# A perceiver layer on one core: the beginning of the score phase by a written plan, projections in pairs, and context parts made a step further ahead

## The chip, the core and the metric

The kernel runs on one core of a Trainium2 chip. TensorE (PE) multiplies, VectorE (DVE) does elementwise arithmetic and reductions, ScalarE (ACT) copies, casts and exponentials, GpSimd (POOL) a few reductions over partitions, SyncE (SP) issues nearly all transfers, which 16 DMA engines carry out. Each engine takes its instructions in the order in which the program gives them to it, and waits on semaphores of the others. The metric is the device time of the whole program in microseconds (us), lower is better: the median of several runs.

## The reference: what is computed

One layer of a perceiver. `x` is 128 rows of 512 numbers, the context is 12544 rows of 512. There are three residual parts:

```python
x = x + cross_attention(layernorm(x), context)      # 16 heads of 128, softmax over 12544 rows
x = x + linear_attention(layernorm(x))              # 16 heads of 32, gated
x = x + ffn(layernorm(x))                           # 512 -> 2048 -> 512, weights and inputs quantized
```

Only the first is touched by the change. Its scores are `(x Wq) (context Wk)^T / sqrt(128)`, for all heads, and its output is `softmax(scores) (context Wv) Wo`.

The kernel never projects the context. It takes Wk to the query side, so that each head's query becomes a vector of 512 numbers, and weighs the raw context with the exponentials before Wv is applied. All large products are done in a fast float32 form with operands split into a high and a low part: `a b` becomes `lo hi + hi lo + hi hi`, three matmuls.

## The kernel before

**Prologue** (lines 171 to 276). The query rows are normalised (`layernorm`, L105), transposed (L198, L199) and projected. Heads are taken in eight pairs, `h2` from 0 to 7. For each pair, `load_w` (L173) loads 512 KB of query weights `wq` and 512 KB of key weights `wk`; `project_q` (L201) makes `pq` in PSUM, and ACT scales it into `qT` (L213); `project_k` (L216) multiplies `qT` with the key weights into `pk`, and ACT copies `pk` out in two halves (L230) into the buffers `b`. There are two buffers for `pq` and two for `pk`. On PE the order is q0, q1, k0, q2, k1, and so on.

The first four head pairs are called f = 0, the other four f = 1. From the `b` of each, seven operands are made for a Strassen-Winograd product: B11, T2, T3, T1, T4, B21, B22 (`operands`, L236). `put` (L232) casts one to its high part on ACT and subtracts it on DVE for the low part. They stay in SBUF, in rooms named `kq0_n` and `kq1_n` for the two f. The other side, the context transposed, comes in pieces of two row blocks: `load_ct` (L147) loads 512 KB, `sum_ct` (L155) makes four sums of it on DVE, `split_ct` (L162) the high parts on ACT and the low parts on DVE.

**Score units** (`scores`, L293). A unit is one context piece i of 49 with one f. It makes seven products of six 128x512 matmuls each (L300), p1, p6, p7, p5, p4, and then p2 added onto p1 and p3 added onto p5 in their PSUM banks. DVE combines them: u2 (L319), u3 (L322), c22 (L325), c21 (L328), c12 (L338); ACT copies p1 out twice (L316, L334). p3 can't begin before DVE has read p5 for c22. The unit's scores, 1 MB, go to DRAM (L339), and DVE keeps a running maximum (L332, L343). During the first units, `more` puts what is left of the f = 1 operands between DVE's steps (L283 to L287, L318 and on). There are 98 units.

**Context steps** (L566 to L606). 196 steps, two to a unit, f = 0 first. Step k takes 24 matmuls (`weigh`, L355, records at L362) with the exponentials of half a unit's scores as one operand (`ph` and `pl`, high and low) and half a context piece as the other (`ch` and `cl`). A step takes PE 24 times 226.7 ns, 5.44 us. Around it, in the order of L586 to L595, stand: `high_part` of step k+2, `cut_hi` (makes `ch`), `low_part` of step k+1 (makes `pl`), `soften` of k+3 (DVE subtracts the maximum, ACT takes the exponential, in place in `si`), `cut_lo` of k+1 (makes `cl`), `total` of k+1 (DVE adds up the denominator `lsum`), the load of the scores of k+5 and that of the context of k+3. `ch`, `cl` and the two loads happen in every other step. `pl` has two buffers. Beside them, jobs are hung on certain steps (`at`, L538), among them a reduction over partitions on POOL (`all_over`, L551) of the f = 0 denominators at step 104.

**Change of phase** (L435 to L469). Before the last unit, `soften`, `cut_hi` and `high_part` of step 0 are given out, and the rest of step 0 and parts of step 1 during it, through `more`. The scores and context of the second pair of steps are loaded after it.

**What sets the order.** Instructions are recorded in the order of the program text, and a scheduler then may move them within each engine; those in `seq(...)` (`keep_in_program_order`, L74) stay in the order in which they are given among themselves. In the prologue and in the units most are free before the change.

**The tail** (L610 and on) does the rest of the layer. The change doesn't touch its text.

Of the kernel before, what the change touches and what calls it, by code (L numbers as in the profile page):

```python
# [8 lines left out]
F32 = mybir.dt.float32  # L9
# [7 lines left out]
P = 128  # L17
# [16 lines left out]
def tile_perceiver_layer(  # L34
# [111 lines left out]

    def load_ct(i):  # L147
        if i == 1:
            raw = kq1p.tile([P, 8, 2, P], F32, name=f"kq1_{B22}")
        else:  # L150
            raw = ctp.tile([P, 8, 2, P], F32, tag="raw", name="ctr", bufs=1)
        nc.sync.dma_start(out=raw[:, A11:, :, :], in_=cT[i])
        return raw

    def sum_ct(raw):  # L155
        r = lambda s: raw[:, s, :, :]
        nc.vector.tensor_tensor(r(S1), r(A21), r(A22), ALU.add)
        nc.vector.tensor_tensor(r(S3), r(A11), r(A21), ALU.subtract)
        nc.vector.tensor_tensor(r(S2), r(S1), r(A11), ALU.subtract)
        seq(nc.vector.tensor_tensor(r(S4), r(A12), r(S2), ALU.subtract))  # L160

    def split_ct(raw, lo=None):  # L162
        hi = ctp.tile([P, 7, 2, P], F32R, tag="hi", name="cth")
        if lo is None:
            lo = ctp.tile([P, 7, 2, P], F32R, tag="lo", name="ctl")
        nc.scalar.copy(hi, raw[:, :7, :, :])
        nc.vector.tensor_tensor(lo, raw[:, :7, :, :], hi, ALU.subtract)
        return hi, lo


    with tc.tile_pool(name="ps_pro", bufs=2, space=PSUM) as ps_pro:

        def load_w(h2):  # L173

            hs = slice(h2 * 256, (h2 + 1) * 256)
            if h2 in (2, 3):
                both = kq1p.tile([P, 2, 1024], F32, name=f"kq1_{h2 + 2}")
                wq = both[:, 0, :].rearrange("p (c e) -> p c e", c=NC)
                wk = both[:, 1, :].rearrange("p (h d) -> p h d", h=2)
            else:  # L180
                wq = ctp.tile([P, NC, 256], F32, tag="hi", name="wq")
                wk = ctp.tile([P, 2, D], F32, tag="lo", name="wk")
            nc.sync.dma_start(out=wq, in_=x_wq[:, hs].rearrange("(c p) e -> p c e", p=P))
            nc.sync.dma_start(out=wk, in_=x_wkT[hs, :].rearrange("(h p) d -> p h d", p=P))
            return wq, wk

        keep_warm(ps_pro, 9)
        ws = [load_w(h2) for h2 in range(4)]
        raw = load_ct(0)
        xn = mxp.tile([P, D], F32, tag="mx1", name="xn")  # L190
        layernorm(xn, x0, D)

        warm = const.tile([P, 1], F32, name="warm")
        seq(nc.scalar.activation(warm, x0[:, 0:1], AF.Exp))
        xnT = tmp.tile([P, NC, P], F32, tag="u3", name="xnT")
        pt = ps_pro.tile([P, NC, P], F32, tag="q", name="pt")
        for i in range(NC):
            nc.tensor.transpose(pt[:, i, :], xn[:, i * P : (i + 1) * P], ident)  # L198
        nc.vector.tensor_copy(xnT, pt)  # L199

        def project_q(h2):  # L201
            pq = ps_pro.tile([P, 2, P], F32, tag="q", name="pq")
            for j in range(2):
                for cc in range(NC):
                    nc.tensor.matmul(  # L205
                        pq[:, j, :],
                        lhsT=ws[h2][0][:, cc, j * HD : (j + 1) * HD],
                        rhs=xnT[:, cc, :],
                        start=(cc == 0),
                        stop=(cc == NC - 1),  # L210
                    )
            qT = tmp.tile([P, 2, P], F32, tag=("p1", "u2")[h2 % 2], name="qT")
            nc.scalar.mul(qT, pq, HD**-0.5)  # L213
            return qT

        def project_k(h2, qT, b):  # L216

            pk = ps_pro.tile([P, 2, 2, 256], F32, tag="k", name="pk")
            for cc in range(NC):
                for j in range(2):  # L220
                    nc.tensor.matmul(  # L221
                        pk[:, cc // 2, cc % 2, j * P : (j + 1) * P],
                        lhsT=ws[h2][1][:, j, cc * P : (cc + 1) * P],
                        rhs=qT[:, j, :],
                        start=True,
                        stop=True,
                    )
            o = h2 % 2 * 256
            for a in range(2):
                nc.scalar.copy(b[h2 // 2 % 2][:, a, :, o : o + 256], pk[:, a, :, :])  # L230

        def put(f, s, v):  # L232
            nc.scalar.copy(right(f, s, 0), v)
            nc.vector.tensor_tensor(right(f, s, 1), v, right(f, s, 0), ALU.subtract)  # L234

        def operands(f, b):  # L236

            (b11, b21), (b12, b22) = ((t[:, 0, :, :], t[:, 1, :, :]) for t in b)
            t2 = mxp.tile([P, 2, 512], F32, tag=f"mx{f}", name="t2")
            sub = lambda out, x, y: nc.vector.tensor_tensor(out, x, y, ALU.subtract)  # L240
            return [
                lambda: sub(b11, b12, b11),
                lambda: sub(t2, b22, b11),
                lambda: put(f, T2, t2),
                lambda: sub(b12, b22, b12),
                lambda: put(f, T3, b12),
                lambda: put(f, T1, b11),
                lambda: sub(b21, b21, t2),
                lambda: put(f, T4, b21),
                lambda: put(f, B22, b22),  # L250
            ]

        qT = project_q(0)
        for h2 in range(8):
            if h2 + 4 < 8:
                ws.append(load_w(h2 + 4))
            if h2 == 1:
                raw1 = load_ct(1)
            nxt = project_q(h2 + 1) if h2 + 1 < 8 else None
            if h2 % 4 == 0:  # L260
                b = [iop.tile([P, 2, 2, 512], F32, tag="io", name="b") for _ in range(2)]
            project_k(h2, qT, b)
            qT = nxt
            if h2 == 1:
                put(0, B11, b[0][:, 0, :, :])
                put(0, B21, b[0][:, 1, :, :])
            if h2 == 2:
                sum_ct(raw)
            if h2 == 3:
                rest = operands(0, b)  # L270
                for do in rest[:6]:
                    do()
            if h2 == 5:
                cts = {0: split_ct(raw, mbp.tile([P, 7, 2, P], F32R, name="mb"))}
                for do in rest[6:]:
                    do()
# [3 lines left out]
    mx = [mxp.tile([P, 1024], F32, name=f"mx{f}") for f in range(2)]  # L280
    psx = ExitStack()
    ps_s = psx.enter_context(tc.tile_pool(name="ps_s", bufs=8, space=PSUM, reuse_waits="tile"))
    beside = operands(1, b)  # L283
    beside[6:6] = [lambda: put(1, B21, b[0][:, 1, :, :])]
    beside[:0] = [
        lambda: (sum_ct(raw1), cts.update({1: split_ct(raw1)})), lambda: put(1, B11, b[0][:, 0, :, :]),
    ]  # L287

    def more():
        if beside:  # L290
            beside.pop(0)()

    def scores(i, f, hi, lo):  # L293


        def product(ps, a, b, first):
            n = 0
            for cc in range(2):
                for lt, part in ((lo, 0), (hi, 1), (hi, 0)):
                    nc.tensor.matmul(  # L300
                        ps, lhsT=lt[:, a, cc, :], rhs=right(f, b, part)[:, cc, :], start=(first and n == 0), stop=(n == 5),
                        skip_group_check=True,
                    )
                    n += 1
            return ps

        def bank():
            return ps_s.tile([P, 512], F32, tag="s", name="ps")

        so = iop.tile([P, 2, 1024], F32, tag="io", name="so")  # L310
        c11, c12, c21, c22 = (so[:, j, b * 512 : (b + 1) * 512] for j in range(2) for b in range(2))
        p1s = tmp.tile([P, 512], F32, tag="p1", name="p1s")
        u2 = tmp.tile([P, 512], F32, tag="u2", name="u2")
        u3 = tmp.tile([P, 512], F32, tag="u3", name="u3")
        p1 = product(bank(), A11, B11, True)
        nc.scalar.copy(p1s, p1)  # L316
        p6 = product(bank(), S2, T2, True)
        more()  # L318
        nc.vector.tensor_tensor(u2, p6, p1s, ALU.add)  # L319
        more()  # L320
        p7 = product(bank(), S3, T3, True)
        nc.vector.tensor_tensor(u3, p7, u2, ALU.add)  # L322
        more()
# [7 lines left out]
        if i > 0 and not late:  # L331
            nc.vector.tensor_tensor(mx[f], mx[f], so[:, 1, :], ALU.max)  # L332
# [675 lines left out]
```

## Time and profile before

| what | value |
|---|---|
| median of 3 runs | 2135.51 us (2135.2 to 2136.2) |
| profiled execution | 2136.68 us |
| its span | 2135.0 us |
| PE busy | 2121.8 us |
| DVE busy | 1658.6 us |
| ACT busy | 762.9 us |
| matmuls L300 on the chain, 4080 | 925.12 us |
| first matmul of the context steps | at 972.74 us |
| first matmul of the tail | at 2040.94 us |
| HBM read and written | 245.77 MB and 103.02 MB |

The profile is that of one execution. Its span is the time from its first to its last instruction, 1.7 us less than the device time of the same execution. Times of single instructions are counted from the span's start. A projection matmul appears as two records on PE, a score or context matmul as one; a record's duration is longer than the distance to the next, because matmuls are pipelined. Idle time of an engine other than PE costs nothing unless PE waits for that engine.

### The profile page before, as it was taken

Reading aid. Unit: us, or ns where it says so; the run is one execution under the profiler, and the core shown is the slowest. Engines: PE = TensorE matmul, PEld = TensorE weight load, DVE = VectorE, ACT = ScalarE, POOL = GpSimd, SP = SyncE. Lnnn points to the kernel's source line nnn. Section 1 sums busy time; section 2 is a strip of 40 time slices with the busy share of each in tenths; the row PEclk is TensorE's granted clock in tenths of the full one; section 3 lists DMA queues with packets and bytes.
Section 4 is the critical chain, followed back from the end, with each engine's and each line's share of the span. In section 5 each row is a group of like instructions: output and inputs, shape, how many; then the busy total and the mean of one; then the engine's idle time right before and its main releaser. Section 6 shows DMA issues by size and latency. Waiting matters only on the chain.

```text
span 2135.0 us, 24185 instructions
## 1 busy us (share of the span) xinstructions
PE 2121.8 (99%) x9627; PEld 1748.9 (82%) x9627; DVE 1658.6 (78%) x1824; ACT 762.9 (36%) x843; POOL 23.5 (1%) x16
## 2 busy tenths in 40 slices
PE   8999999999999999999999999999999999999999
PEld 7888888888888888888888888888888888888885
DVE  6877777777777777778997888877787777777735
ACT  5222122221222212215444444444544444444423
POOL 0000000000000000000000000000000000000010
PEclk9999999999999999999999999999999999999999
DMA  6444443444444444446664555554434444444460
GB/s 221 150 170 160 173 178 154 166 160 170 178 152 171 159 168 178 158 158 227 211 230 152 176 178 180 194 182 144 148 138 140 146 148 148 148 142 145 147 191 25
DMA packets 77393, 350.36 MB, mean 164 GB/s; under 512 B 8000, under 2 KB 12352, under 8 KB 51808
## 3 DMA queue, kind: packets, MB, share of 16 engines
q1 hardware_dynamic: 77136, 348.69, 45.5%
q8 instruction: 75, 1.23, 0.2%
q14 instruction: 38, 0.31, 0.0%
q10 hardware_dynamic: 144, 0.13, 0.0%
HBM read 245.77 MB, written 103.02 MB: 163 GB/s over the span
## 4 chain that ended last, share of the span: by engine, by line
PE 97%; DVE 2%; DMA 1%; issue 1%; ACT 0%; DVEq 0%; SPq 0%
PE pu L362 49%; PE ps L300 43%; PE pw L92 1%; PE pc L631 1%; PE po L652 0%; DMA kq<-in_cT_dram 0%; PE pp L742 0%; DVE kq L234 0%; DMA kq<-in_a_wq_dram 0%; PE pq L205 0%; DVE b L240 0%; PE po L795 0%; PE py L939 0%; PE pk L221 0%; PE pv L766 0%
## 5 line engine op out<-in xcount | busy, mean ns | idle before, releaser
L300 PE MATMUL ps<-kq,cth 128*128 128x512 f32 x2744 | 844.9, 389 | 0.0
L362 PE MATMUL pu<-ph,cl 128*128 128x512 f32 x1568 | 610.2, 389 | 1.4 <-DVE cl L404 1.2
L362 PE MATMUL pu<-ph,ch 128*128 128x512 f32 x1568 | 610.0, 389 | 0.0
L362 PE MATMUL pu<-pl,ch 128*128 128x512 f32 x1568 | 610.0, 389 | 0.0
L300 PEld LDWEIGHTS ps<-kq,cth 128*128 128x128 f32 x2744 | 515.2, 188 | 106.7
L300 PE MATMUL ps<-kq,ctl 128*128 128x512 f32 x1344 | 522.8, 389 | 0.0
L421 DVE TENSOR_TENSOR pl<-si,ph 128x1024 fp32r<-128x1024 f32 x194 | 241.3, 1244 | 203.3 <-PE pu L362 201.6
L362 PEld LDWEIGHTS pu<-ph,cl 128*128 128x128 f32 x1568 | 294.3, 188 | 63.2 <-DVE cl L404 2.2
L362 PEld LDWEIGHTS pu<-pl,ch 128*128 128x128 f32 x1568 | 294.3, 188 | 61.2
L362 PEld LDWEIGHTS pu<-ph,ch 128*128 128x128 f32 x1568 | 294.3, 188 | 61.0
L416 ACT CAST ph<-si 128x1024 fp32r<-128x1024 f32 x194 | 204.0, 1051 | 389.6 <-PE pu L362 389.5
L300 PEld LDWEIGHTS ps<-kq,ctl 128*128 128x128 f32 x1344 | 252.3, 188 | 52.4
L334 ACT COPY so<-ps 128x512 f32<-128x512 f32 x98 | 57.8, 589 | 577.0 <-PE ps L300 577.0
L411 ACT ACTIVATE si<-si 128x1024 f32<-128x1024 f32 x194 | 205.3, 1058 | 116.7 <-DVE si L410 116.7
L410 DVE TENSOR_TENSOR si<-si,mb 128x1024 f32<-128x1024 f32 x194 | 236.6, 1220 | 0.0
L429 DVE TENSOR_TENSOR lsum<-lsum,si 128x1024 f32<-128x1024 f32 x192 | 234.1, 1219 | 0.0
L338 DVE TENSOR_TENSOR so<-ps,u 128x512 f32<-128x512 f32 x98 | 67.8, 691 | 72.3 <-PE ps L300 72.3
L343 DVE TENSOR_TENSOR mx<-mx,so 128x1024 f32<-128x1024 f32 x95 | 116.4, 1225 | 9.6
L404 DVE TENSOR_TENSOR cl<-cr,ch 128x1024 fp32r<-128x1024 f32 x98 | 119.6, 1220 | 0.5 <-ACT ch L398 0.5
L332 DVE TENSOR_TENSOR mx<-mx,so 128x1024 f32<-128x1024 f32 x95 | 116.5, 1227 | 3.2
L398 ACT CAST ch<-cr 128x1024 fp32r<-128x1024 f32 x98 | 103.3, 1054 | 40.8 <-DMA cr<-in_c_dram 40.8
L328 DVE TENSOR_TENSOR so<-ps,u 128x512 f32<-128x512 f32 x98 | 67.7, 691 | 61.2 <-PE ps L300 61.2
(203 smaller groups left out, 1012.4 us busy)
## 6 DMA issues: line engine op xcount, KB each, us to landing
sc<-so SPq DMA_DIRECT2D x98, 1024.0 KB, 3.8
si<-sc SPq DMA_DIRECT2D x97, 1024.0 KB, 4.8
cr<-in_c_dram SPq DMA_DIRECT2D x98, 512.0 KB, 3.5
ctr<-in_cT_dram SPq DMA_DIRECT2D x94, 512.0 KB, 3.5
kq<-in_w1T_dram SPq DMA_DIRECT2D x16, 512.0 KB, 4.8
kq<-in_w2T_dram SPq DMA_DIRECT2D x16, 512.0 KB, 4.9
wq<-in_x_wq_dram SPq DMA_DIRECT2D x6, 512.0 KB, 5.4
wk<-in_x_wkT_dram SPq DMA_DIRECT2D x6, 512.0 KB, 6.2
```

What stands on the lines that cost most here:

```text
L300: nc.tensor.matmul(ps, lhsT=lt[:, a, cc, :], rhs=right(f, b, part)[:, cc, :], start=(first and n == 0), stop=(n == 5), skip_group_check=True,)
L332: nc.vector.tensor_tensor(mx[f], mx[f], so[:, 1, :], ALU.max)
L338: nc.vector.tensor_tensor(c12, p5, u2, ALU.add)
L343: nc.vector.tensor_tensor(mx[f], so[:, 1, :] if i == 0 else mx[f], so[:, 0, :], ALU.max)
L362: nc.tensor.matmul(pu[b][cc], lhsT=lt[:, j, cs], rhs=rt[:, bs], start=(first and n == 0), stop=(last and n == 2))
L398: seq(nc.scalar.copy(ctx_hi[f, i], ctx_raw[f, i]))
L404: seq(nc.vector.tensor_tensor(ctx_lo[f, i], ctx_raw[f, i], ctx_hi[f, i], ALU.subtract))
L410: seq(nc.vector.tensor_tensor(exps[k], exps[k], mb[f], ALU.subtract))
L411: seq(nc.scalar.activation(exps[k], exps[k], AF.Exp))
L416: seq(nc.scalar.copy(high[k], exps[k]))
L421: seq(nc.vector.tensor_tensor(low[k], exps[k], high[k], ALU.subtract))
L429: seq(nc.vector.tensor_tensor(lsum[f], lsum[f], exps[k], ALU.add))
```

## The change

The prologue and the first four units, (0,0), (1,0), (0,1), (1,1) as (i, f), are no longer placed by the scheduler: a text names every step, each step is a small function, and all are kept in the order of the text. Six things differ:

1. The normalisation is written out: two halves of 256 columns, transposed into two PSUM buffers, the first copied out by ACT, the second by DVE.
2. Projections come in pairs on PE: q0 q1 k0 k1 q2 q3 k2 k3 and so on. The copies out of `pk`, called c0a, c0b to c7a, c7b, are placed one by one, some of them much later.
3. The loads are issued in another order: wq0, wq1, wk0, wk1, then wq2, wk2, the first context piece, wq3, wk3, then wq4, wk4, the second context piece, and the rest. The weights of pairs 2, 3, 5 and 6 go to rooms that f = 1 operands will take later, wq7 to that of a maximum; the last block of f = 1 is kept in the room of T4. 
4. The units' body becomes a table of named steps (`unit`); the later units run through it in the order as before.
5. At the change of phase, `soften` and `high_part` of step 1 come before the last unit, `cut_lo` of step 0, `low_part` of steps 0 and 1 within it, and the loads of the second pair of steps before and within it.
6. In the context steps `low_part` and `cut_lo` work for step k+2 instead of k+1, `pl` has three buffers, and the context is loaded for k+4 instead of k+3.

The context piece of a unit is now kept in `raws`, so that it is loaded once for both f; before, from i = 2 on, it was loaded again for f = 1 (L450).

The plan, and the steps that it names (cut to the core; `put` and `operands` of before became the steps h.., l.. and T..):

```diff
+    plan = """
+        q0 q1 qT0 k0 qT1 k1 c0a c0b q2 c1b hB210 lB210 q3 qT2 c1a hB110 S01 S00 k2 S02 qT3 lB110 S03 k3 c2b c2a hi0
+        S11 q4 S10 S12 S13 c3b lo0 ct2 c3a q5 qT4 hB220 T10 k4 qT5 hi1 T30 k5 T20 hT10 lo1 hT30 q6 c4b c5a T40 q7 qT6
+        hT20 lB220 c5b k6 lT20 qT7 hT40 lT30 k7 c6a lT40 c6b c4a lT10 u00p1 c7a hB111 u00p6 c7b lB111 hB221 u00p7 T11
+        u00p1s u00U2 hT11 u00p5 u00U3 hB211 u00p4 u00c22 T21 u00p2 u00c21 hT21 T31 u00p3 u00c11 lT21 hT31 u10p1 u00c12
+        lT31 u10p6 u10p1s lB221 u10p7 u10U2 u10p5 u10U3 S20 u10p4 u10c22 lB211 u10p2 T41 u10p3 u10c21 hT41 lT11 u10c11
+        u01p1 lT41 u01p6 u01p1s u10c12 u00m2 u01p7 u01U2 u01p5 u01U3 S22 u01p4 u01c22 S21 S23 u01p2 u01c21 u10m1 u01p3
+        u01c11 u10m2 u11p1 hi2 u01c12 u01m2 u11p6 u11p1s lo2 u11p7 u11U2 u11p5 u11U3 u11p4 u11c22 u11p2 u11c21 u11m1
+        u11p3 u11c11 u11c12 u11m2
+    """
...
+        room = {2: B11, 3: B21, 5: T3, 6: T1}
+        if h2 in room:
+            both = spare(room[h2], [P, 2, 1024])
...
+            if h2 == 7:
+                wq = mxp.tile([P, NC, 256], F32, tag="mx1", name="wq")
...
+    ws = [load_w(h2) for h2 in range(4)]
+    begin(ws[0][2][0], ws[1][2][0], ws[0][2][1], ws[1][2][1], *ws[2][2])
+    raws[0] = load_ct(0)
+    begin(*ws[3][2])
...
+    for half in range(2):
+        hs = slice(half * 256, (half + 1) * 256)
+        seq(nc.vector.tensor_scalar(xn[:, hs], x0[:, hs], mv[:, 0:1], r, ALU.subtract, ALU.mult))
+    for half in range(2):
+        pt = ps_pro.tile([P, 2, P], F32, tag="q", name="pt")
+        for n in range(2):
+            c0 = (2 * half + n) * P
+            seq(nc.tensor.transpose(pt[:, n, :], xn[:, c0 : c0 + P], ident))
+        to = xnT[:, 2 * half : 2 * half + 2, :]
+        seq(nc.vector.tensor_copy(to, pt) if half else nc.scalar.copy(to, pt))
...
+    for h2 in range(4, 8):
+        ws.append(load_w(h2))
+        begin(*ws[h2][2])
+        if h2 == 4:
+            raws[1] = load_ct(1)
...
+    def leave(h2, a):
+        o = h2 % 2 * 256
+        seq(nc.scalar.copy(block(h2 // 2, a)[:, :, o : o + 256], pks[h2][:, a, :, :]))
...
+    for name in plan.split():
+        if name == "u00p1":
+            pro.close()
+            ps_s = psx.enter_context(tc.tile_pool(name="ps_s", bufs=8, space=PSUM, reuse_waits="tile"))
+        steps_.pop(name)()
```

The change of phase and the context steps:

```diff
     def low_part(k):
         if k < len(steps):
-            low[k] = weigh_operand("pl", 2)
+            low[k] = weigh_operand("pl", 3)
...
+            load_scores(2)
             soften(0)
             cut_hi(0)
             high_part(0)
-            beside = [
-                lambda: None, lambda: None, lambda: cut_lo(0), lambda: None,
-                lambda: low_part(0), lambda: (soften(1), high_part(1)),
-            ]
-        if i + 1 not in cts and i + 1 < NP and i > 0:
-            raw = load_ct(i + 1)
...
+            soften(1)
+            high_part(1)
+            beside = {
+                "U2": [lambda: cut_lo(0), lambda: load_ctx(2)],
+                "c22": [lambda: low_part(0)],
+                "c21": [lambda: low_part(1)],
+            }
+        if i + 1 not in cts and i + 1 < NP and i + 1 not in raws:
+            raws[i + 1] = load_ct(i + 1)
...
-    load_scores(2)
-    load_ctx(2)
...
+        soften(2)
         total(0)
-        soften(2)
         load_scores(4)
...
             high_part(k + 2)
             cut_hi(k + 2)
-            low_part(k + 1)
             soften(k + 3)
-            cut_lo(k + 1)
+            cut_lo(k + 2)
+            low_part(k + 2)
             total(k + 1)
...
             load_scores(k + 5)
-            load_ctx(k + 3)
+            load_ctx(k + 4)
```

## The prediction

> **What bounds the kernel now.** I read the page first: span, then busy shares.
>
> ```profile
> span 2135.0 us, 24185 instructions
> PE 2121.8 (99%) x9627; PEld 1748.9 (82%) x9627; DVE 1658.6 (78%) x1824; ACT 762.9 (36%) x843; POOL 23.5 (1%) x16
> ```
>
> TensorE (PE) is busy for all but 13.2 us. Its matmul count is the same after the change (no matmul is added or removed), and in the steady stretches 128x512 matmuls follow each other every 226.7 ns whatever the other engines do (chain: 4080 of L300 in 925.12 us). So the change can only move PE's idle time. The waits of PE, longest first, say whom it waited for, in us:
>
> ```profile
> PE pk L221 <- ACT qT L213: 1.4, 1, 1.4
> ...
> PE pu L362 <- DVE cl L404: 1.2, 1, 1.2
> PE ps L300 <- ACT b L230: 1.0, 1, 1.0
> PE pq L205 <- DVE xnT L199: 0.8, 1, 0.8
> ...
> PE ps L300 <- DVE so L325: 0.7, 1, 0.7
> ```
>
> Each happens once. The timeline of PE (start, duration, in brackets the idle time before) places them:
>
> ```profile
> 7.10 3.84 PE L205 MATMUL pq<-xnT,wq 128*128 128x128 f32 x32 [0.78 <-DVE xnT L199]
> ...
> 35.56 2.05 PE L221 MATMUL pk<-qT,wk 128*128 128x128 f32 x16 [1.39 <-ACT qT L213]
> ...
> 40.03 0.50 PE L300 MATMUL ps<-kq,mb 128*128 128x512 f32 x1 [1.02 <-ACT b L230]
> ...
> 47.79 0.50 PE L300 MATMUL ps<-kq,mb 128*128 128x512 f32 x1 [0.66 <-DVE so L325]
> ```
>
> Measured from start to start (idle time counts from modelled ends, and the first matmul after a wait takes 0.11 longer), they cost: before the last key projection 35.56-34.01 = 1.55; before the second product 1.42-0.23+0.11 = 1.30; before the seventh product 1.05-0.23+0.11 = 0.93. Later two more: at 983.41 to 983.94, 0.53-0.23+0.11 = 0.41, and at 1549.60 to 1551.20, 1.60-0.23+0.11 = 1.48. The last one's reason is in the timelines of POOL and DVE:
>
> ```profile
> 1543.26 6.12 POOL L554 PARTITION_ALL_REDUCE mb<-lsum  x1 [94.77 <-DVE lsum L553]
> ```
>
> ```profile
> 1544.43 4.45 DVE L421 TENSOR_TENSOR pl<-si,ph 128x1024 fp32r<-128x1024 f32 x1 [1.34 <-PE pu L362]
> 1548.80 1.21 DVE L410 TENSOR_TENSOR si<-si,mb 128x1024 f32<-128x1024 f32 x1
> 1549.94 1.21 DVE L404 TENSOR_TENSOR cl<-cr,ch 128x1024 fp32r<-128x1024 f32 x1
> ```
>
> The same subtraction usually takes 1.22; beside the reduction it took 4.45, and `cl`, third in the queue, came too late. All these waits together with a later start are 0.75+1.55+1.30+0.93+0.41+1.48 = 6.4 us (the 0.75 is worked out below): the ceiling, 0.30%. Last, the transfers of the first 70 us (40 slices of 1.75 us, busy tenths and rate):
>
> ```profile
> DMA  0899999999999918827207271000095000292000
> GB/s 0 262 358 314 354 384 381 367 396 365 372 372 372 298 65 270 240 98 219 81 0 211 89 229 70 0 0 0 0 374 225 9 5 0 112 407 84 0 0 0
> ```
>
> They are saturated up to 24.5. Issue plus time to landing gives, in order of issue: 3.5 (x), 5.0, 7.1, 8.8, 10.1, 11.6, 13.0, 14.5, 15.8, 17.1, 18.6, 20.6, 22.1, 23.4, 24.7. A load of 512 KB lands every 1.5 us on average, in order of issue, whether it is a query weight, a key weight or context.
>
> **What the Trainium skill says.** "TensorE: Matmul & The Clock Gate", section "Architectural detail: the array is 16× 32×32, not 1× 128×128", calls ScalarE and VectorE strict FIFO; the trace agrees: `qT` of the last pair ran at 35.10, behind a 1.70 us cast and three more, though its input had been ready since 32.3. "SBUF — State Buffer", section "Who interferes with whom", says that a `tensor_tensor` with both inputs in SBUF contends with GpSimd's reads and that the one to issue second blocks; 4.45 for 1.22 agrees. "DMA: Bandwidth & Descriptors", section "Queues, rings and completion order", says that descriptors of a ring are consumed in order; the landings agree.
>
> **The change, part by part.** A projection is 16 records, 1.785 us (start to start, 8.90 to 10.69 and on). I follow PE.
>
> Start. The normalisation goes in halves, and so do transpose and copy. The kernel's own later layer does this already (L731, L717): from the first half's start (2070.94) transposes start after 0.47, ScalarE's copy after 0.94 and ends after 1.31. From 5.00 this gives 6.31, first projection at 6.35 instead of 7.10: 0.75 earlier. The other half's copy, on DVE, ends after 1.69, at 6.69; PE needs it after four more matmuls, at 7.24.
>
> Projections. New order q0 q1 k0 k1 q2 q3 k2 k3 and on; loads in the order wq0 wq1 wk0 wk1 wq2 wk2 ct0 wq3 wk3 wq4 wk4 ct1 wq5 wk5 wq6 wk6 wq7 wk7. Five projections end at 6.35+8.93 = 15.28, each load there in time. q3 needs the ninth load, 15.81: it starts at 15.85, 0.57 of waiting. q3 k2 k3 q4 end at 22.99; q5 needs the fourteenth load, 23.40: 0.46 more. q5 k4 k5 q6 q7 end at 23.45+8.93 = 32.38. So the transfers eat 1.03, more than the earlier start gave. On SP's queue the moved loads wait for: wq4 q0 (8.1; it was issued at 9.18 before), wk4 k0 (11.7; 12.76 before). Five loads are then still outstanding, and the others take rooms of the second pair's operands, which wait for no matmul. So the queue stays full, and I keep the landings by position.
>
> Last projections, from ScalarE's new queue. k6 takes the PSUM room of k5, and c5b, which empties it, stands behind qT6 and hT20. q6 ends at 30.59; qT6 starts at 30.79 (copies start 0.31 after the last record's start), holds the queue for 0.28, hT20 for 0.95, c5b takes 0.59: 32.61, k6 at 32.65. k7 takes the room of k6 in turn: k6 ends at 34.43, c6a starts at 34.63, c6b at 35.11 and ends at 35.70: k7 at 35.74, a wait of 1.31 that was not there, in place of the 1.55 for `qT`. Then k7 to 37.62, first product to 38.98. The second product needs the bank that c7b empties, behind c7a (0.48) and hB111 (0.95): 37.82+1.43+0.59 = 39.84, so it starts at 39.9. Before it started at 40.03. From there on: the seventh product waits for c22 on DVE. DVE now has only u2, u3 and c22 (0.69 each) between the fifth product's end, about 44.3, and its need at 46.8, so the 0.93 go. The second pair's operands are due from 57.6 on; DVE's nine remaining passes of 1.14 fit between 45 and 60, the last due at 63. Prologue: 0.13+0.93 = 1.06 gained.
>
> Change of phase (983). `si`, `ch`, `ph`, `pl` of steps 0 and 1 move into the last score unit, and two loads ahead of it. `cl` of step 2 then stands fourth in DVE's row after the last unit instead of ninth (the row from 973.54) and ends near 979; PE needs it at 971.7+10.9 = 982.6. The work moved fills DVE's idle time in that unit (0.74 at 972.9, 0.45 at 968.6, 0.32 at 967.5); the subtractions of steps 0 and 1 now stand ahead of u2, and with the same durations c22 of that unit still ends 0.7 before its need. Gain 0.41.
>
> Context steps. `cl` and `pl` are made two steps ahead instead of one, with a third `pl` buffer. In an ordinary step `cl` ended 3.5 us into a step of 5.44 (1524.95+1.22 against PE's release at 1522.67), 1.9 to spare; the reduction costs DVE 3.23, hence the wait. With another step of 5.44 to spare it is covered: gain 1.48. DVE's work per step is unchanged (3 or 4 passes of 1.14). The context load now follows its reader in the same step and has 10 us; it had about 5.
>
> Context for the scores is loaded once per pair instead of twice (46 loads of 512 KB fewer). Hidden before and after: no wait on it is listed on PE. Worth 0.
>
> Sum: 1.06+0.41+1.48 = 2.95. The profiled execution took 2136.68 (span 2135.0 and 1.7 around it); 2133.7 after. The median of the runs is 2135.51; after it 2132.6, a gain of 0.14%.
>
> **Rivals.** *Loads no limit.* If the ninth and fourteenth load land 1 us earlier than by position, the 1.03 goes, less what ScalarE's order gives back: 3.9 us, 2131.6; with one of the two PSUM waits (1.31, 0.9) halved as well it passes 4.3, 2130.8. For it: the first loads ramp up slowly. Against: 370 GB/s throughout.
>
> *Loads later.* From q3 on PE has no slack against them, so each microsecond costs one. Landings 2.95 later than by position make the kernel slower than before; 7.2 later by over 0.2%, some 2140. Speaks for it: SP is one queue, and wk4, which waits for k0, stands ahead of ten loads; the twelfth load took 2.0. Against: 7 us of transfers are queued when it is issued.
>
> *The lead is not real.* `cl` also waits for the room of the pair before, free only when PE enters the step. If DVE gets no further ahead, 1.48 stays: 2134.0. Against: the room is free a full two steps before the need.
>
> *The prologue gives nothing* and only the 1.9 of the later phases remain: 2133.6.
>
> **How the numbers follow.** Likeliest (0.62): 1.5 to 4.2 us gained. Faster rival 0.17; lead or prologue void 0.15; slower 0.06. 0.2% is 4.3 us, about what a measurement of this kernel can tell from no change: so faster 0.17, within 0.77, slower 0.06. Range: down to 2130.4, which leaves 0.10 of the faster case out, and up to 2135.3, which leaves the slower case and little else. The tail's half-clock stretch (granted clock 0.50 from 2090.08 to 2096.9) can fall otherwise; the three runs span 1.0, inside the range.
>
> **What would show it.** Right: PE's waits of `qT`, `so` and `cl` gone from the list; in their place a wait on a query load near 15, one near 23, one on the copy out of `pk` near 35 (1.3) and one near 39 (0.8); second product at 39.9; first `pu` at 971.7 instead of 972.74; none at 980 or 1550. Wrong: PE reaching the second product before 38.5 (loads no limit) or after 42 (loads late), or a new wait inside the units.

## The result, and the profile after

| what | before | after |
|---|---|---|
| median | 2135.73 us (22 runs, 2133.36 to 2137.95) | 2131.53 us (22 runs, 2129.99 to 2134.30) |
| ratio after to before | | 0.9984, 95% interval 0.9978 to 0.9990 |
| profiled execution, its span | 2136.68, 2135.0 | 2134.19, 2132.5 |
| first matmul of the context steps | 972.74 | 974.19 |
| from there to the first matmul of the tail | 1068.20 | 1066.24 |
| tail (from there to the end) | 94.0 (6.83 us of it at half clock) | 92.0 (3.41 us of it at half clock) |
| HBM read | 245.77 MB | 221.65 MB |

The change takes 0.16% off: 3.4 us by the ratio, 4.2 by the medians, where 2.95 were forecast. That is more than forecast, and still less than 0.2%.

The profiled execution of the kernel after took 2.7 us more than the median, and its first context matmul comes *later* than before. Read alone it would say that the whole prologue was a loss. The page comes first: the same number of matmuls, 1.7 us less PE time, 11.1 us less of DVE.

```profile
span 2132.5 us, 23984 instructions
...
PE 2120.1 (99%) x9627; PEld 1748.0 (82%) x9627; DVE 1647.5 (77%) x1825; ACT 753.9 (35%) x844; POOL 26.1 (1%) x16
```

PE's list of waits after (us in total, times, longest):

```profile
PE pq L344 <- DMA kq<-in_x_wq_dram: 2.0, 2, 1.1
...
PE pk L364 <- ACT kq L384: 1.2, 1, 1.2
PE ps L190 <- ACT kq L384: 0.7, 1, 0.7
PE pq L344 <- DMA wq<-in_x_wq_dram: 0.5, 1, 0.5
PE pp L851 <- DMA kq<-in_a_wq_dram: 0.5, 1, 0.5
...
PE pk L364 <- ACT b L384: 0.2, 1, 0.2
```

The waits on `qT`, `cl` and `so` of before are gone. In their place stand waits on query loads, and on ScalarE's copies out of `pk` (L384). PE's timeline places them (start, duration, in brackets the idle time before):

```profile
6.44 2.05 PE L344 MATMUL pq<-xnT,wq 128*128 128x128 f32 x16 [0.20 <-ACT xnT L327]
8.97 2.02 PE L344 MATMUL pq<-xnT,wq 128*128 128x128 f32 x16 [0.48 <-DMA wq<-in_x_wq_dram]
...
17.32 2.02 PE L344 MATMUL pq<-xnT,kq 128*128 128x128 f32 x16 [0.96 <-DMA kq<-in_x_wq_dram]
...
25.75 2.02 PE L344 MATMUL pq<-xnT,kq 128*128 128x128 f32 x16 [1.05 <-DMA kq<-in_x_wq_dram]
...
35.09 2.05 PE L364 MATMUL pk<-qT,kq 128*128 128x128 f32 x16 [0.17 <-ACT b L384]
38.30 2.05 PE L364 MATMUL pk<-qT,wk 128*128 128x128 f32 x16 [1.16 <-ACT kq L384]
40.11 0.47 PE L190 MATMUL ps<-kq,mb 128*128 128x512 f32 x1
...
42.46 0.50 PE L190 MATMUL ps<-kq,mb 128*128 128x512 f32 x1 [0.72 <-ACT kq L384]
```

These are the forecast's waits at the forecast's places (q3, q5, k6, k7, second product), plus one at q1 (8.97) that it had not. The load waits came out at about double the size, and the second product at 42.46 instead of 39.9; the prediction had named "after 42 (loads late)" as a sign of being wrong, and this execution shows it. After it PE has no gap until the context steps, none at 983 and none at 1550. The reduction and the subtraction beside it are still there, the reduction first, DVE's row after it:

```profile
1546.50 6.95 POOL L663 PARTITION_ALL_REDUCE mb<-lsum  x1 [93.86 <-DVE lsum L662]
```

```profile
1547.39 5.56 DVE L528 TENSOR_TENSOR pl<-si,ph 128x1024 fp32r<-128x1024 f32 x1
1552.87 1.21 DVE L536 TENSOR_TENSOR lsum<-lsum,si 128x1024 f32<-128x1024 f32 x1
```

The subtraction takes 5.56 us (4.45 before, 1.22 elsewhere), and nobody waits for it.

### The profile page after: what moved, and what is told of

It is laid out like the page before. It is cut to its first block, busy times and chain, and to the rows that moved or that the text cites. A ratio compares the mean times of both kernels' runs of the same rounds, so it can differ in the third digit from the quotient of the medians.

```text
span 2132.5 us, 23984 instructions
## 1 busy us (share of the span) xinstructions
PE 2120.1 (99%) x9627; PEld 1748.0 (82%) x9627; DVE 1647.5 (77%) x1825; ACT 753.9 (35%) x844; POOL 26.1 (1%) x16
## 3 DMA queue, kind: packets, MB, share of 16 engines
q8 instruction: 75, 1.23, 0.2%
HBM read 221.65 MB, written 103.02 MB: 152 GB/s over the span
## 4 chain that ended last, share of the span: by engine, by line
PE 98%; DMA 1%; DVE 0%; ACT 0%; issue 0%; SPq 0%; DVEq 0%; ACTq 0%
PE pu L469 50%; PE ps L190 44%; PE pw L92 1%; PE pc L740 1%; DMA kq<-in_x_wq_dram 1%; PE po L761 0%; PE pk L364 0%; PE pp L851 0%; DMA wq<-in_x_wq_dram 0%; DMA kq<-in_a_wq_dram 0%; PE pq L344 0%; PE po L904 0%; PE py L1048 0%; PE pv L875 0%; PE pw L1018 0%; PE pp L930 0%
## 5 line engine op out<-in xcount | busy, mean ns | idle before, releaser
L219 DVE TENSOR_TENSOR so<-ps,u 128x512 f32<-128x512 f32 x294 | 202.9, 690 | 134.8 <-PE ps L190 130.4
L176 DVE TENSOR_TENSOR ctl<-ctr,cth 128x1792 fp32r<-128x1792 f32 x47 | 94.9, 2019 | 0.7 <-ACT cth L171 0.7
L171 ACT CAST cth<-ctr 128x1792 fp32r<-128x1792 f32 x48 | 81.7, 1703 | 37.5 <-PE ps L190 35.4
```

The lines of the kernel that those rows point to most:

```text
L176: return lo, nc.vector.tensor_tensor(lo, raw[:, :7, :, :], hi, ALU.subtract)
L219: place(nc.vector.tensor_tensor(to, t[p], t[q], ALU.add))
```

## The experiments

**What is compared.** The effects are near 1 us and single runs of one kernel span 4, so each comparison is given twice: by medians and the ratio, and by the mean span of those runs whose mean granted clock is 1.000. The second number needs a sentence: in some executions TensorE's granted clock falls to half for 3.41 or 6.83 us in the tail, which lengthens the tail (below) and shows as a mean clock of 0.999 or 0.998. This is the table that the rest rests on (the runs of before from all comparisons together; the intervals are 95%, from the scatter alone):

| kernel | mean span at clock 1.000 (runs) | against before |
|---|---|---|
| before | 2132.94 (38) | |
| `e1_context`: before with parts 5 and 6 | 2130.70 (9) | -2.24 ± 0.39 |
| `e2_prologue`: after without parts 5 and 6 | 2131.91 (8) | -1.03 ± 0.41 |
| after | 2129.29 (14) | -3.66 ± 0.29 |
| `e7_order`: after, first loads in the old order | 2129.40 (8) | -3.54 ± 0.45 |
| `e3_fewer`: after, two loads fewer | 2128.28 (6) | -4.66 ± 0.31 |
| `e4_rooms`: after, five copies earlier | 2127.22 (4) | -5.72 ± 0.37 |
| `e8_rooms_order`: both edits | 2126.72 (6) | -6.23 ± 0.53 |

**The two halves of the change, one at a time.** `e1_context` puts the lead and the new change of phase into the kernel before:

```diff
-            low[k] = weigh_operand("pl", 2)
+            low[k] = weigh_operand("pl", 3)
...
-            low_part(k + 1)
...
-            cut_lo(k + 1)
+            cut_lo(k + 2)
+            low_part(k + 2)
...
-            load_ctx(k + 3)
+            load_ctx(k + 4)
```

and at the change of phase gives out the same steps early, through `more`. `e2_prologue` is the kernel after with these lines the other way round.

> The kernel before with the change of phase and the context steps of the change alone; prologue and units as before. Both theories: the waits at 983 (0.41 us) and at 1550 (1.48) go, nothing else moves before the tail. First context matmul at 972.7 as before, first matmul of the tail 1.9 earlier, at 2039.0. The total then follows the tail: 1.9 us faster if the tail takes what it took in the kernel before (94.1 from its first matmul to the end), up to 3.9 if its half-clock stretch shortens from 6.8 to 3.4 us as in the profile of the changed kernel. Rival (the lead is not real): the wait at 1550 stays at 1.2 or more and the tail starts 0.4 earlier.

> The changed kernel with the change of phase and the context steps put back: prologue, units and single context loads of the change alone. Theory A (the profile of the changed kernel is typical: its loads land up to 2.2 us later than by position): second product at 42.4, first context matmul at 974.2, 1.4 us slower than before. Theory B (that execution was unusually late; ordinarily loads land by position): second product at 39.9 to 40.5, first context matmul at 971.7 to 972.3, 0.5 to 1.1 us faster than before. In both the waits at 983 and 1550 are there again.

Measured: `e1_context` 2133.35 us, ratio 0.9991 (0.9984 to 0.9998); `e2_prologue` 2133.84, ratio 0.9992 (0.9984 to 1.0000). In the trace of the first the gap at 1550 is gone and the context steps take 1066.66 us instead of 1068.20: 1.54 less. A new gap of 0.37 takes most of what the missing one at 983 gave: the seventh matmul of step 0 starts only at 974.33, when VectorE has read the last unit's c12 (L338, 973.59 to 974.27), which now stands behind the `low_part` of step 1 in VectorE's row. In the kernel after, where the last unit gives out these steps in its own order, that gap is missing too and the steps take 1066.24, which is 196 times 24 times 226.67 ns: PE without a pause. In the trace of `e2_prologue` the wait for `cl` is back, beside the two copy waits:

```profile
PE pu L469 <- DVE cl L511: 1.2, 1, 1.2
PE pk L364 <- ACT kq L384: 1.2, 1, 1.2
PE pq L344 <- DMA kq<-in_x_wq_dram: 1.0, 1, 1.0
PE ps L190 <- ACT kq L384: 0.7, 1, 0.7
```

Its second product at 41.43 and first context matmul at 973.17 lie between the two theories (42.4 and 974.2, 39.9 to 40.5 and 971.7 to 972.3). Both halves gain, and -2.24 and -1.03 add up to the -3.66 of the whole within their intervals. But 2.24 is 0.7 more than the trace of the context steps shows, so where the gains arise has to be asked of the stages; see the tail, below.

**Is it the reduction that made `cl` late?** `e5_noreduce` is the kernel before without it: VectorE copies the denominators onto themselves in its place, so that the f = 0 outputs are divided by sums of one partition only.

```diff
-    at(2 * NP + 6, lambda: all_over(rl[0], lsum[0], bass_isa.ReduceOp.add))
+    at(2 * NP + 6, lambda: seq(nc.vector.tensor_copy(lsum[0], lsum[0])))
```

> The kernel before, without the reduction over partitions on POOL of the f = 0 denominators at step 104 (a DVE copy of the denominators onto themselves stands in its place, so the f = 0 outputs are divided by sums of one partition only). Theory A (the reduction holds DVE up, and so cl comes late): the subtraction of the low part near 1544.4 takes 1.22 us again instead of 4.45, PE has no gap near 1550, the rest as before; 1.5 us faster, too little for one look at the time, so the trace decides. Theory B (the gap at 1550 comes from the jobs of those steps, not from the reduction): the gap of about 1.6 us stays.

DVE's timeline there:

```profile
1545.11 1.23 DVE L421 TENSOR_TENSOR pl<-si,ph 128x1024 fp32r<-128x1024 f32 x1 [1.34 <-PE pu L362]
1546.26 1.22 DVE L410 TENSOR_TENSOR si<-si,mb 128x1024 f32<-128x1024 f32 x1
1547.39 1.22 DVE L404 TENSOR_TENSOR cl<-cr,ch 128x1024 fp32r<-128x1024 f32 x1
```

The subtraction takes 1.23, `cl` ends at 1548.6, PE steps through 1550 every 0.227, and the context steps take 1066.69 us instead of 1068.20. So the reduction was the cause, and the lead is a cover for it, not a cure: with the lead, the subtraction beside it takes even longer (5.56).

**What limits the new prologue: loads or copies?** `e3_fewer` leaves out the two loads of the fourth head pair, which takes the weights of the third (these two heads are computed with the weights of two others).

```diff
-    ws = [load_w(h2) for h2 in range(4)]
+    ws = [load_w(h2) for h2 in range(3)]
+    ws.append(ws[2])
...
-    begin(*ws[3][2])
```

`e4_rooms` changes only the plan: five copies out of `pk` go ahead of casts and other work on ScalarE, so that PSUM rooms come free earlier.

```diff
-        S11 q4 S10 S12 S13 c3b lo0 ct2 c3a q5 qT4 hB220 T10 k4 qT5 hi1 T30 k5 T20 hT10 lo1 hT30 q6 c4b c5a T40 q7 qT6
-        hT20 lB220 c5b k6 lT20 qT7 hT40 lT30 k7 c6a lT40 c6b c4a lT10 u00p1 c7a hB111 u00p6 c7b lB111 hB221 u00p7 T11
+        S11 q4 S10 S12 S13 c3b lo0 ct2 c3a q5 qT4 hB220 T10 k4 qT5 hi1 c4a c4b T30 k5 T20 hT10 lo1 c5a c5b hT30 q6 T40 q7 qT6
+        hT20 lB220 k6 lT20 qT7 hT40 lT30 k7 c6a lT40 c6b lT10 u00p1 c7a c7b hB111 u00p6 lB111 hB221 u00p7 T11
```

> The changed kernel without the two loads of the fourth pair: that pair takes the weights of the third, so a part of the projections is of other data. Everything behind them in the queue moves up two places, some 3 us. If loads set the pace of the projections: the waits for wq3 and wq5 (0.96 and 1.05 us in the profile of the changed kernel) go to 0, the second product moves from 42.5 to about 39.0 to 40.0, and the total falls by 1.0 (by position) to 3 us. If they do not: second product where it was and the same time. The waits on ScalarE's copies before k7 (1.16) and the second product (0.72) stay in both.

> The changed kernel with one edit of the plan: the copies c4a, c4b, c5a, c5b come right after k4 and k5 and c7b ahead of hB111, so that k6 and k7 find the PSUM rooms of k4 and k5 empty and the second product its bank. My theory: the waits on ScalarE's copies (0.17, 1.16 and 0.72 us idle, with restarts 0.38, 1.26 and 1.05) go, 2.7 us faster than the changed kernel, second product at 39.8 where the changed one has 42.5, and no new wait. Rival (ScalarE is full, and the wait moves on): one of qT6, qT7, the casts of T2 or T4 comes late instead, and less than 1 us is gained.

Measured: `e3_fewer` 2130.44 us, ratio 0.9977 (0.9967 to 0.9986); `e4_rooms` 2129.20, ratio 0.9969 (0.9957 to 0.9981). In `e3_fewer` the load waits of q3 and q5 are gone (the matmuls of q2 and q3 follow each other, first line), the three copy waits stay, and the second product stands at 40.02:

```profile
14.45 3.74 PE L344 MATMUL pq<-xnT,kq 128*128 128x128 f32 x32
...
32.64 2.05 PE L364 MATMUL pk<-qT,kq 128*128 128x128 f32 x16 [0.17 <-ACT b L384]
35.86 2.05 PE L364 MATMUL pk<-qT,wk 128*128 128x128 f32 x16 [1.16 <-ACT kq L384]
...
40.02 0.51 PE L190 MATMUL ps<-kq,mb 128*128 128x512 f32 x1 [0.72 <-ACT kq L384]
```

In `e4_rooms` the three copy waits are gone, and the load wait of q3 stays (that of q5 is missing in this execution):

```profile
16.68 2.02 PE L344 MATMUL pq<-xnT,kq 128*128 128x128 f32 x16 [0.97 <-DMA kq<-in_x_wq_dram]
...
32.88 1.95 PE L364 MATMUL pk<-qT,kq 128*128 128x128 f32 x16
34.67 1.95 PE L364 MATMUL pk<-qT,wk 128*128 128x128 f32 x16
36.38 0.47 PE L190 MATMUL ps<-kq,mb 128*128 128x512 f32 x1
```

The last two key projections and the products follow without a pause, the second product at 37.85. The copies were worth 2.06 us by the table (5.72 - 3.66), where 2.7 were expected, and the two loads 1.00: two separate limits, and ScalarE's order is the larger. With the plan's lines changed the kernel is faster than both, before and after.

**Why did the loads land later than by position?** In the first profiles two query weights at the head (wq0, wq1) went with a third load at 8.2 to 9.1 us, and wq0, wk0, wq1 with 7.09 in the kernel before (though with 7.75 in `e1_context`, where the expectation below says 7.1). So the order of issue was suspected, and put back, in the kernel after (`e7_order`) and in that with the earlier copies (`e8_rooms_order`):

```diff
-    begin(ws[0][2][0], ws[1][2][0], ws[0][2][1], ws[1][2][1], *ws[2][2])
+    begin(*ws[0][2], *ws[1][2], *ws[2][2])
```

The rival was the execution itself; both kernels were therefore profiled again, unchanged.

> The kernel after, with the first four weight loads in the order of the kernel before: wq0 wk0 wq1 wk1 instead of wq0 wq1 wk0 wk1. In every kernel profiled so far with two query weights at the head, the third load (x is the first) landed at 8.2 to 9.1 us and all later ones about 1.4 later than by position; in those with wq0 wk0 wq1 it landed at 7.1. Theory A (two query weights in a row cost one load slot): third load near 7.1, ninth near 15.8, fourteenth near 23.4; waits on loads before q3 and q5 about half of those of the kernel after; first matmul of the context steps near 971.6 instead of 974.19; about 2130 us, 1.0 to 2.5 faster than the kernel after. Theory B (what came late was not the order but the execution): third load at 8.2 or later again, first matmul of the context steps at 973 to 974, time as the kernel after, 2131.5.

> The kernel with the copies c4a c4b, c5a c5b and c7b placed earlier, and the first four loads in the order wq0 wk0 wq1 wk1 as well. Theory A: third load near 7.1, ninth near 15.8; PE reaches the second product near 37.1 instead of 37.85, the first matmul of the context steps stands near 968.8 instead of 969.51; about 2128.5 us. Theory B: landings and times as with the earlier copies alone, 2129.2.

> The kernel before, unchanged, profiled a second time: do the landings of the first loads vary from execution to execution of one program? Theory B (they do): the third load lands anywhere from 7.1 to 9.1 us, not again within 0.2 of the 7.09 of the first profile; where it is later than 8.2, PE waits for a query load near 9 as well and the first matmul of the context steps moves from 972.74 to about 973.4. Theory A (they are set by the program): 7.1 again, later loads within 0.2 of the first profile.

> The kernel after, unchanged, profiled a second time. Theory B: the third load again late (8 to 9), but the lost slot at the thirteenth load (24.20 where 22.8 would follow its neighbours) is gone, so that PE has one wait of about 1 us for a query load instead of two beside the one near 9, and the first matmul of the context steps stands near 973.1 instead of 974.19. Theory A: 24.2 and 974.2 again.

> The kernel before once more. So far its prologue put the first matmul of the context steps at 972.7, 972.7, 973.4 and 974.0 us, depending on where the loads lost time. Theory B: again within 972.7 to 974.0. Which part of a run at full clock makes up the mean span of 2132.9 is asked: with 1068.2 for the context steps and 90.6 for the tail the first context matmul stands at 974.1; with a tail of 91.6 as in the second look, at 973.1.

> The kernel after once more. Its runs at full clock have a mean span of 2129.3; with 1066.24 for the context steps and a tail of 90.5 the first context matmul stands at 972.5, which no profile has shown yet (974.19, 973.13). Theory A, the prologue's gain of 1.0 to 1.4 stands in the start of the context steps: 971.7 to 972.7 here, with the waits on loads no longer than the predicted 0.57 and 0.46. Theory B, it does not: 973 to 974 again.

> As the look before it, a third draw: 971.7 to 972.7 by theory A, 973 to 974 by theory B. The three waits on copies by ScalarE (0.2, 1.2, 0.7) stand in each by both.

Measured: `e7_order` 2132.31 us, ratio 0.9986 (0.9980 to 0.9993), no better than the kernel after; `e8_rooms_order` 2128.96, ratio 0.9973 (0.9964 to 0.9983), not to be told from `e4_rooms`. In us, from the traces:

| profile | third load | ninth | fourteenth | first context matmul |
|---|---|---|---|---|
| before | 7.09 | 15.81 | 23.40 | 972.74 |
| before, second profile | 7.85 | 16.25 | 24.68 | 974.00 |
| before, third profile | 8.11 | 16.50 | 23.47 | 972.79 |
| `e5_noreduce` (prologue of before) | 8.81 | 17.36 | 24.14 | 973.43 |
| `e1_context` (prologue of before) | 7.75 | 16.24 | 23.39 | 972.70 |
| after | 8.84 | 17.18 | 25.62 | 974.19 |
| after, second profile | 7.89 | 16.20 | 23.89 | 973.13 |
| after, third profile | 6.92 | 16.08 | 23.76 | 972.34 |
| after, fourth profile | 8.05 | 16.80 | 23.74 | 972.54 |
| `e2_prologue` (prologue of after) | 9.09 | 17.44 | 24.47 | 973.17 |
| `e7_order` | 8.73 | 17.21 | 24.25 | 973.07 |
| `e8_rooms_order` | 7.84 | 16.30 | 24.84 | 970.61 |

The order theory falls: with the old order the third load landed at 8.73 and 7.84, and the old prologue has it anywhere from 7.09 to 8.81. One program loses up to 2 us at the third load, or 0.6 to 1.5 at the twelfth or thirteenth, in one execution and not in the next. The third profile of the kernel after is of an execution in which little was lost. In its timeline the loads make PE wait 0.56 and 0.29 and the copies what they did:

```profile
16.22 2.02 PE L344 MATMUL pq<-xnT,kq 128*128 128x128 f32 x16 [0.56 <-DMA kq<-in_x_wq_dram]
...
23.89 2.02 PE L344 MATMUL pq<-xnT,kq 128*128 128x128 f32 x16 [0.29 <-DMA kq<-in_x_wq_dram]
...
33.23 2.05 PE L364 MATMUL pk<-qT,kq 128*128 128x128 f32 x16 [0.17 <-ACT b L384]
36.45 2.05 PE L364 MATMUL pk<-qT,wk 128*128 128x128 f32 x16 [1.16 <-ACT kq L384]
...
40.61 0.50 PE L190 MATMUL ps<-kq,mb 128*128 128x512 f32 x1 [0.73 <-ACT kq L384]
```

The second profile of the kernel after has its first context matmul where it was expected (973.1), but not for the reason expected: PE waits for no load in it, and its first projection ran at half clock (below).

In the kernel before, one load alone decides. The last key projection waits for `qT`, but the chain behind it starts at the landing of the second context piece, the fifteenth load, and goes on through VectorE's row up to the c22 for which the seventh product waits. From its critical chain:

```profile
16.75 7.97 DMA kq<-in_cT_dram
...
24.74 0.42 DVE kq L157
...
47.05 0.69 DVE so L325
...
47.79 925.12 PE ps L300 x4080
```

In all five profiles with the old prologue that load landed at 24.72, 25.97, 24.74, 25.42 and 24.69 (in the order of the table), the seventh product started 23.1 later and the first context matmul 948.0 later. So a delay of PE ahead of it is absorbed: in `e5_noreduce` PE waits 1.2 for the third load and then 0.6 instead of 1.4 for `qT`; in the third profile of before the clock rose late, the first projection started at 7.62 instead of 7.10, and the wait for `qT` is 0.7. In the second profile the fifteenth load itself came 1.25 later, and the whole was paid:

```profile
36.81 2.05 PE L221 MATMUL pk<-qT,wk 128*128 128x128 f32 x16 [1.54 <-ACT qT L213]
```

The prediction counted the waits for `qT`, for the copy out of `pk` and for c22 one by one and didn't name this chain. In the kernel after, the second context piece is the thirteenth load, and it is not on the chain.

What in the transfers loses the time stays open. The exact size of the prologue's own gain stays open too. The first context matmul averages 973.13 in the five profiles with the old prologue and 973.07 in the six of the table with the new one (`e8_rooms_order` left out), 0.06 apart with a scatter of near 2. The timed runs give 1.03 ± 0.41 (`e2_prologue`), which may all be the tail's (below), and 1.42 ± 0.42 (after against `e1_context`, 3.66 - 2.24), of which 0.42 lie in the context steps (1066.66 - 1066.24). That leaves anything from nothing to about 1 us.

**The tail.** With the clock full to the end, the tail takes 91.56 and 91.75 us in the two later profiles of the kernel before, and 90.52, 90.53, 90.65 and 90.54 in the third and fourth profile of after, in `e1_context` and in `e2_prologue`. The difference is a wait for the query weights of the second part of the layer (`a_wq`). First the third profile of the kernel before, then the third of the kernel after:

```profile
2073.35 7.38 PE L742 MATMUL pp<-xaT,kq 128*128 128x128 f32 x64 [1.14 <-DMA kq<-in_a_wq_dram]
```

```profile
2069.94 7.41 PE L851 MATMUL pp<-xaT,kq 128*128 128x128 f32 x64
```

The load is issued 24.85 and 24.84 us into the tail in these two, and is under way 7.4 us in one and 5.5 in the other. All four profiles with the context steps of before and its prologue have the wait (0.5, 0.9, 1.1, 0.8). Of the kernel after, one of four has it (0.5); the six other kernels with one half of the change or all of it, `e1_context` and `e2_prologue` among them, have none. If the timed runs are like these profiles, the tail is worth 1.1, which covers the 0.7 that `e1_context` gained beyond its context steps, and all of the 1.03 of `e2_prologue`. The rate of the transfers from 4 us before its issue to 9 after, 40 slices of 0.325 us, first in the third profile of before, then in that of after:

```profile
GB/s 328 277 277 302 328 221 227 227 296 429 366 347 384 353 365 384 265 309 353 366 347 340 315 372 334 158 132 189 246 315 214 258 359 378 384 378 397 347 183 158
```

```profile
GB/s 378 403 101 0 6 57 25 57 151 378 384 416 416 410 397 378 240 132 365 277 397 416 391 416 403 290 120 25 246 384 328 403 397 410 403 403 107 25 25 0
```

In the second the queue runs all but empty 3 us before the issue (101, 0, 6, 57), in the first it never does, so the load probably stands behind others there. That this makes it late was not tested, and which edit changes it was not isolated.

The other thing that moves a tail is the clock. With half clock for 3.41 us the tail of after is 91.75 (second profile), in `e4_rooms` with 6.83 us 93.40, against 90.53 with none: 1.2 and 2.9 us. The Trainium skill, "TensorE: Matmul & The Clock Gate", section "What's actually happening", gives the window in which activity is counted as 3413 ns and calls it free-running. The stretches that end before the program does agree with it: they last 3.413 us or twice that, whatever the kernel, and they begin 2078.72, 2082.13 or 2085.54 us after the clock rose, which is 609, 610 or 611 times 3.413. When the clock rises at the start varies as well, from 4.54 to 10.49 us in the profiles; in the second profile of after it was 10.49, so that its first projection took 3.6 us instead of 1.8.

## Why the prediction was right, point by point

**Sign and size.** Forecast 2.95 gained, 1.06 in the prologue and 1.89 in the later phases. Measured 3.4 by the ratio, 3.66 ± 0.29 at full clock. The third and fourth profile of after against the second and third of before (all at full clock, mean spans 2129.20 and 2133.25) split 4.05 into 0.95 before the context steps (973.39 to 972.44), 1.96 in them and 1.13 in the tail (91.66 to 90.53). The middle term is firm. The first hangs on which executions were drawn (0.06 over all profiles), and the third was not forecast. So that the total came so near is in part luck: the tail gave about what the prologue may have fallen short.

**Context steps and change of phase: right.** 1.48 + 0.41 forecast, 1.96 measured; the rival that the lead is not real falls. The reduction as cause was shown by taking it away, the lead as cover by the 5.56 that nobody waits for.

**Copies behind ScalarE's queue: right.** In the profile of the kernel after, start to start, with the 1.785 of a projection: k6 35.09 - 32.97 - 1.785 = 0.34 (forecast 0.27), k7 38.30 - 35.09 - 1.785 = 1.43 (1.31), second product 42.46 - 40.11 - 1.36 = 0.99 (0.92). That they limit was shown by `e4_rooms`. The places where PE then stands were not met: the second product at 40.61 to 42.46 in the profiles of after where 39.9 was forecast, the first context matmul at 972.34 to 974.19 where 971.7 was.

**The start: right in kind, 0.1 to 0.2 smaller.** q0 at 6.44 to 6.58 instead of the forecast 6.35 where the clock was up in time. **The seventh product: right**; its wait is missing in every profile with the new prologue. It was the end of VectorE's chain from the second context piece.

**Loads: right in place, mis-sized.** The step that failed is "I keep the landings by position", which took one profile of before as the landing times. The waits of 0.57 and 0.46 came out as 0.56 and 0.29 in one execution, as 1.16 and none in another, as none at all in the one whose clock rose late, and as 0.96 and 1.05, with 0.48 at q1 in addition, in the one profiled first. The 1.00 ± 0.34 that the two loads are worth on average by `e3_fewer` is near what was forecast as their sum, 1.03; it was the trust in one sample that was wrong. "From q3 on PE has no slack against them, so each microsecond costs one" held: in the first profile of after the ninth and fourteenth load came 1.1 and 1.9 later than in the third, the first context matmul 1.85 later.

**The tail: missing.** It was listed as a thing that can fall otherwise, by the clock alone. The wait on `a_wq`, 0.5 in the profile of before, was on the list of waits that it read, and was not followed. The 1.1 of the tail is about the difference between 2132.6 and 2131.53.

**The rivals.** "Loads no limit" falls with `e3_fewer` (the loads cost 1.00), "the lead is not real" with the context steps. "The prologue gives nothing" stays open: the time measured is 2 us below its 2133.6, but 1.1 of this are the tail's, and what `e2_prologue` gained can be the tail's as well. "Loads later" came true in part, in single executions and by 1 to 2 us, less than the 2.95 from which it would have decided; but the loads of before are as late in other draws, so little of it is a difference between the kernels.

## What to carry to other kernels

A chain of PE, loads and an in-order engine has more than one limit at once: taking PE's visible waits away brings up the next. And several waits on different engines can hang on one chain, as three did here on the landing of one load; follow each back before adding them up. Read from the queue of the copying engine which buffer comes free when, and put the copies that free PSUM ahead of work that is due later; here that was worth another 2 us, more than the rewritten prologue itself, which gave about 1 at most.

Landing times of one profile are one draw. Where an engine runs without slack against loads, profile the same program several times before a landing time goes into a sum, and compare the single stages of executions with the same granted clock.

A lead of one more step, for one more buffer, hides a rare collision (here a reduction on GpSimd that stretches a VectorE subtraction from 1.2 to 5.6 us). Whether another order within the step would do it too was not tried.

## What the runs showed of the hardware that was not expected

- The same load of 512 KB, third in its queue, landed between 6.92 and 8.84 us in four executions of one program, and in one of them another 1.4 us were lost at the thirteenth (24.20 where the loads before it lead to 22.8).
- The subtraction beside GpSimd's reduction took 4.45 us in the kernel before, 5.56 in the kernel after and 5.55 in `e1_context`, and the reduction 6.12, 6.95 and 6.94. By the profile it ended 0.5 us before the reduction each time (1548.88 and 1549.38 in the kernel before), so it was slowed, and did not wait for all of it.
- A half-clock stretch of 3.41 us in the tail costs 1.2 us of time, one of 6.83 us 2.9.
